# S4 convolution gated by a LoRA feed-forward: the first block's loads on two queues, 20 identity products instead of 24, and VectorE sums at other places of the order

## The chip, the cores and the metric

The kernel runs on one core of one Trainium2 chip, in float32. The metric is the device time of one execution in microseconds (us). A core has TensorE (PE in the profile; its weight loads are PEld), VectorE (DVE), ScalarE (ACT), GpSimd (POOL) and SyncE (SP), whose queue issues most of the DMAs here. ScalarE has a DMA queue of its own. Each engine works through its own list of instructions in order and waits on semaphores.

## The reference, cut to what matters

```python
# x: (2, 1024, 512); w1, w3: (1376, 512); w2: (512, 1376); LoRA rank 16, scale 2
xn = layernorm(x)                                   # no affine, eps 1e-5
s = causal_conv(xn, K) + D * xn                     # along the last axis; K of 512 taps from the S4 state
h1 = xn @ w1.T + 2 * (xn @ A1.T) @ B1.T
h3 = xn @ w3.T + 2 * (xn @ A3.T) @ B3.T
g = silu(h1) * h3
f = g @ w2.T + 2 * (g @ A2.T) @ B2.T
out = x + s * silu(f)
```

The convolution runs over the 512 features of a token, so as a matrix it is a 512 x 512 Toeplitz matrix. Its taps K come from a Cauchy sum at 512 roots and an inverse Fourier transform, computed in the kernel from small inputs.

## The kernel before

**Tiling.** The 2048 tokens are four blocks of 512 tokens, each loaded as four tiles of 128 x 512. A block is normalized (bn_stats and bn_aggr on VectorE for blocks 0 to 2, ScalarE sums for block 3, then one scale and shift per row on ScalarE and GpSimd) and transposed on TensorE into `xr` and `b12`, with ScalarE copying the transposes out of PSUM.

**First product.** `h1` and `h3` are made with a two-level Strassen-Winograd scheme. The 1376 hidden columns are five pairs of 256 columns (`c` = 0 to 4) and a rest of 96 (`last`). A pair has seven inner products, its chains (`j` = 1, 2, 6, 7, 5, 3, 4 in that order), and each chain has seven steps of two 128x512 matmul instructions. The LoRA term is added to the weights first: a rank 16 product into PSUM (`lora_product`, L381) and a VectorE merge (L391). VectorE makes the sums of weights (`inner_weight_sum`, L451, written S1 to S4 in the scheme, into `s[5]`, `s[6]`, `s[7]`, `s[3]`) and of tokens, and adds each chain's second PSUM accumulation to a snapshot that ScalarE has copied out (`Chain.total`, L778). A `y` bank of PSUM that a chain goes on accumulating in, or that a later chain takes over, is free once that total has read it. GpSimd adds and multiplies results (L868, L835), and the gated `g` goes to DRAM.

**Second product.** `f` is made in eight units of 128 tokens per half (`u` = 0 to 7), two to a group of `g`, one level of Strassen-Winograd. A group's sums (`group_piece`, L1176, eight VectorE instructions) are dropped between the steps of the units before. Units 2 and 3 run while the third group's sums are made, while its `g` comes from DRAM, and while VectorE works off the S4 chain (`s4_work`: `s4_resolvent`, `s4_roots`, `s4_matrix`): a Cauchy resolvent `den`, roots on TensorE (L639) read by L648, small complex arithmetic on 128x4 tiles (L655), the operands `z` of the transform (L688, L690) and their products on TensorE (L709). The convolution of the later units (`conv_product`, L928) needs its result.

**Order.** The order on PE, DVE, ACT and POOL is written out by hand: a heap of places (`at`, `after`) is emptied in order for the first product, where one unit of a place is one step of a chain, and `run` goes through the second product. `run` lets two units take turns; after each step it takes one entry of `parts` and then, from the step `s4_from` on, `s4_steps` entries of `s4_work`. An entry `nothing` does nothing and takes one turn.

**The start.** `load_x(0)` issues the four tiles of block 0 on SP; the LoRA factors for `w1` and `w3` (`lo_d`, `lo_h`, 16 rows each) go out on ScalarE's queue at the same time. SP goes on with block 1, the weights of `last`, the first pair's weights, blocks 2 and 3 and the second pair's weights. Each DMA uses one of eight semaphores in turn, so the ninth waits for the landing of the first. TensorE meanwhile multiplies the identity with itself (`keep_warm`, L989: 24 products, two instructions each), then makes the LoRA products of `last` (`lora_last`, L381), ten more identity instructions, and the transposes of block 0 (L303).

Of the kernel before, what the change touches and what calls it, by code (L numbers as in the profile page):

```python
# [17 lines left out]
P = 128  # L18
# [3 lines left out]
HID = 1376  # L22
# [4 lines left out]
TB = 512  # L27
# [6 lines left out]
LSPLIT = 6 * P  # L34
# [73 lines left out]
def s4_gated_ffn(  # L108
# [39 lines left out]
    nc = tc.nc  # L148
# [19 lines left out]
    def bank(tag, borrow=False):  # L168

        i = turn[tag]  # L170
        if not borrow:
            turn[tag] = 1 - i
        return psum.tile([P, 512], F32, tag=f"{tag}{i}", name=tag, bufs=1)
# [36 lines left out]
    def value(tag="s"):  # L210
        return upool.tile([P, TB], F32, tag=tag, name=tag, bufs={"s": 10, "c": 4}[tag])
# [4 lines left out]
    def at(place, what):  # L216
        heapq.heappush(events, (place, next(count), what))
# [7 lines left out]
    def load_x(b):  # L225
        room = (None, None, t_in[4], t_in[6])[b]
        tiles = []
        for tt in range(NTT):
            t = value() if room is None else room[:, tt, :]
            nc.sync.dma_start(out=t, in_=x[bass.ds(b * TB + tt * P, P), :])  # L230
            tiles.append(t)
        return tiles

# [133 lines left out]
    def load_lora(queue, group, d, h, lo, hi):  # L367
        rows = slice(32 * group, 32 * group + R)
        if d is not None:
            queue.dma_start(out=lora["d"][rows, :], in_=d)  # L370
        queue.dma_start(out=lora["h"][rows, : hi - lo], in_=h[:, lo:hi])
        lora["base"][group] = lo
# [21 lines left out]
    def load_pair(c):  # L394
        w = wpool.tile([P, 8, 2, 2, P], F32, tag="w", name="w")
        for v, src in enumerate((w1T, w3T)):
            for half in range(2):
                slot = (1, 2, 0, 3)[2 * v + half]
                rows = src[half * HALF : (half + 1) * HALF, PAIR_AT[c] : PAIR_AT[c] + 2 * P]
                nc.sync.dma_start(  # L400
                    out=w[:, slot].rearrange("p k m h -> p k (m h)"),
                    in_=rows.rearrange("(k p) h -> p k h", p=P),
                )
        return w
# [12 lines left out]
    def merge_whole_pair(c, w, first=None, delays=(1.15, 2.3, 4.3, 4.4)):  # L417

        ps = [first or [bank("y", True), bank("w", True)], [bank("aux"), bank("aux")]]
        for half in range(2):  # L420
            for k in range(2):
                for v in range(2):
                    n = slice(half * 2 * P, (half + 1) * 2 * P)
                    lora_product(
                        ps[k][v][:, n], 2 * k + v, 2 * half + k, PAIR_AT[c], 2 * P, half == 0
                    )
        for (k, v), when in zip(((0, 0), (0, 1), (1, 0), (1, 1)), delays):
            to = w[:, (slice(1, 3), slice(0, 4, 3))[v], k].rearrange("p s m h -> p s (m h)")
            from_ = ps[k][v].rearrange("p (s n) -> p s n", s=2)
            after(when, lambda to=to, from_=from_: merge(to, from_))  # L430

    def outer_weight_sums(w, names):
        a21, a11, a12, a22, s1, s2, s3, s4_ = (
            w[:, i].rearrange("p k m h -> p (k m h)") for i in range(8)
        )
        sums = {1: (s1, a21, a22, add), 2: (s2, a22, s3, sub), 3: (s3, a11, a21, sub)}
        sums[4] = (s4_, a12, s2, sub)
        for name in names:
            nc.vector.tensor_tensor(*sums[name])  # L439

    def inner_weight_sum(w, s, name):
        a11, a12, a21, a22 = (w[:, 1:, k, m, :] for m in range(2) for k in range(2))
        j = {1: 5, 2: 6, 3: 7, 4: 3}[name]
        s[j] = upool.tile([P, 7, P], F32, tag=f"s{j}", name=f"s{j}")
        first, second, op = {
            1: (a21, a22, add),
            2: (s.get(5), a11, sub),
            3: (a11, a21, sub),
            4: (a12, s.get(6), sub),
        }[name]  # L450
        nc.vector.tensor_tensor(s[j], first, second, op)  # L451
# [21 lines left out]
    def lora_last():  # L473
        ps = [bank("y"), bank("y")]
        for dc in range(NDC):
            for v in range(2):
                lora_product(
                    ps[v][:, dc * LASTR : (dc + 1) * LASTR], v, dc, LAST * P, LASTR
                )
        return ps  # L480
# [283 lines left out]
    class Chain:  # L764
# [16 lines left out]
        def step(self, i):  # L781

            rows = self.rows
            if i == 1:
                self.x = bank("x")[:rows, :]
            elif i == 7:
                self.y = bank("y")[:rows, :]
            to = self.w if i == 2 else self.y if i in (7, 4) else self.x
            product(to, self.pairs(i), i in (1, 7), self.parts if i == 1 else 1)
            if i == 1:  # L790
                self.w = bank("w")[:rows, :]
                nc.scalar.copy(self.w, self.x)  # L792
            elif i == 2:
                after(1.2 + self.late, lambda: self.got(11, self.w))
            elif i == 6:
                self.s2 = self.snapshot(21)
            elif i == 5:
                s4_ = self.snapshot(22)
                after(2.1 + self.late, lambda: self.total(22, s4_))
            elif i == 3:  # L800
                after(1.2 + self.late, lambda: self.got(12, self.x))
            elif i == 4:
                after(1.2 + self.late, lambda: self.total(21, self.s2))
# [163 lines left out]
    lora_tiles(LSPLIT)  # L967
    factors = (a1, b1T), (a3, b3T)
    for v, f in enumerate(factors):
        load_lora(nc.scalar, v, *f, LSPLIT, HID)  # L970
    nc.scalar.activation(warm, warm, AF.Silu)
    x_in[1] = load_x(1)
    make_upper_triangular(nc, tri, 1.0, diag=True)
    w_last, s_last = load_last()
# [12 lines left out]
    def keep_warm(ps, n, first=False):  # L987
        for i in range(n):
            nc.tensor.matmul(  # L989
                ps[:, i % 4 * P : (i % 4 + 1) * P],  # L990
                lhsT=ident,
                rhs=ident,
                start=first and i == 0,
                stop=True,
                skip_group_check=True,
            )

    primed = bank("w"), bank("w")
    for ps in primed:
        keep_warm(ps, 12, True)  # L1000
    ps_last = lora_last()
    mv = norm_tile(0)
    norm_stats(0, range(NTT))
# [73 lines left out]
    for n, place in enumerate((12.1, 12.8, 13.7, 14.4)):  # L1077
        b, i = divmod(n, 2)
# [19 lines left out]
    for c in range(NPAIR):  # L1098
        t0 = 14 + 49 * c

        def ready(j):

            n = orders[c].index(j)
            return 7 * (n + (2 if c == 0 and n > 1 else 0)) + (0 if c == 0 else t0) + 13.3

        if c + 1 < NPAIR:
            nx = c + 1

            def step(what, *args, nx=nx):
                return lambda: what(nx, w_pair[nx], *args)  # L1110

            if c > 0:
                at(t0 + 7.5, lambda nx=nx: w_pair.update({nx: load_pair(nx)}))
            t1 = t0 + (24 if c == 0 else 16)
            if c == 0:
                at(
                    5.7,
                    lambda nx=nx: merge_whole_pair(
                        nx, w_pair[nx], [bank("w"), bank("w")], (1.6, 2.6, 4.8, 5.8)
                    ),  # L1120
                )
            else:
                at(t0 + 15.6, step(merge_whole_pair))
            for n, name in enumerate((3, 2, 1, 4)):
                at(
                    14.5 + 0.2 * n if c == 0 else t1 + 8.5 + 1.5 * n,
                    lambda nx=nx, name=name: outer_weight_sums(w_pair[nx], (name,)),
                )
            for name, when in (
                (3, ready(7)),  # L1130
                (1, ready(5)),
                (2, ready(5) + 4),
                (4, max(ready(3), ready(5) + 8)),
            ):
                at(
                    when,
                    lambda nx=nx, name=name: inner_weight_sum(w_pair[nx], s_pair[nx], name),
                )
        else:
            at(t0 - 20, load_w2_factors)  # L1140
            at(t0 + 5, load_w2)
            for n, when in enumerate((15.6, 22.6, 29.6)):
                at(t0 + when, lambda n=n: merge_down(n))
# [303 lines left out]
    after_, more = following(1)  # L1447
    nothing = [lambda: None]
# [36 lines left out]
    def hold(u):  # L1485
# [5 lines left out]
    after_, more = following(2)  # L1491
    hold(HOLD)
    run(
        [unit(2, read), unit(3, read)],
        [*nothing * 2, *more],
        8,
    )
    for _ in s4_work:
# [1 line left out]
    for u in range(HOLD, UNITS):  # L1500
# [9 lines left out]
        more = ()  # L1510
        if u == HOLD:
            more = nothing + [lambda of=of: [part() for part in of] for of in block_sums_[2:]]
        if ahead and j == 1:
            after_, more = following(grp + 1)
# [77 lines left out]
```

## Time and profile before

| | us |
| --- | --- |
| median of 3 runs | 445.49 |
| lowest and highest run | 444.5 and 445.88 |
| profiled execution, device time | 446.04 |
| its span, first to last instruction | 444.2 |

The profiled execution lies 1.84 us over its own span, and 0.55 us above the median of the runs. Over the whole span TensorE is busy for 437.1 us, VectorE for 318.0, GpSimd for 206.1 and ScalarE for 144.6; 53.61 MB go through the DMA queues. A line of the timeline gives start, duration, engine, source line, operation, what is written and read, and how many instructions are merged in it; the bracket tells how long the engine was idle before, and what ended that. "busy" for TensorE includes the time in which its pipeline drains, so small losses show as a longer distance between starts and not as idle time.

### The profile page before, as it was taken

To read this page: it belongs to the slowest core of one execution; us is meant where nothing else is said; L and a number is where in the kernel's file an instruction comes from. 1 tells how busy PE (TensorE), PEld (TensorE's weight loads), DVE (VectorE), ACT (ScalarE), POOL (GpSimd) and SP (SyncE) were. 2 spreads that over 40 slices of the span, in tenths; PEclk is the share of its full clock that TensorE was granted. 3 is DMA by queue.
4 is the path that set the end of the run, shared out by engine and by line. 5 is a ranking of instruction groups with operands and counts; after the bars stand their busy time and mean duration, and the time that the engine had idled before them with its cause. 6 is when DMAs were issued, how large, how long until landed. Compare 5 with 4: busy or idle time off the path is not lost.

```text
span 444.2 us, 5192 instructions
## 1 busy us (share of the span) xinstructions
PE 437.1 (98%) x1722; PEld 271.8 (61%) x1722; DVE 318.0 (72%) x534; ACT 144.6 (33%) x296; POOL 206.1 (46%) x156
## 2 busy tenths in 40 slices
PE   8999999999999999999999999999999999999996
PEld 8645333344444444444443447888888999999995
DVE  5799999955984687468745796979595885653234
ACT  2676332543254325532453242111101212212221
POOL 2306469895669467945794469400000122222221
PEclk9999999999999999999999999999999999999999
DMA  8911304025102500260036526395901843323211
GB/s 263 364 51 38 136 0 147 0 76 174 37 24 72 165 24 24 76 180 25 24 123 209 163 91 213 106 357 187 346 19 72 281 141 96 142 95 96 78 65 48
DMA packets 35466, 53.61 MB, mean 121 GB/s; under 512 B 4688, under 2 KB 21520, under 8 KB 35312
## 3 DMA queue, kind: packets, MB, share of 16 engines
q1 hardware_dynamic: 35312, 53.14, 36.6%
q8 instruction: 13, 0.21, 0.2%
q10 hardware_dynamic: 128, 0.14, 0.1%
q14 instruction: 13, 0.11, 0.1%
HBM read 33.88 MB, written 19.40 MB: 120 GB/s over the span
## 4 chain that ended last, share of the span: by engine, by line
PE 70%; DVE 18%; DMA 7%; issue 2%; ACT 1%; SPq 1%; DVEq 0%; ACTq 0%
PE x L754 35%; PE y L754 18%; PE w L754 9%; PE aux L928 4%; PE w L928 2%; DVE xt L327 2%; DVE s L1176 2%; DVE w L439 1%; DMA t_in<-g_dram 1%; DMA g<-g_dram 1%; DMA t_in<-in_x_dram 1%; DMA lo_h<-in_b1T_dram 1%; DMA w<-in_w1T_dram 1%; DVE t_in L341 1%; DVE s L451 1%
## 5 line engine op out<-in xcount | busy, mean ns | idle before, releaser
L1310 POOL TENSOR_TENSOR o<-o,xin 128x512 f32<-128x512 f32 (+1 forms) x17 | 23.3, 1370 | 134.3 <-DVE o L1309 134.3
L835 POOL TENSOR_TENSOR s<-c,s 128x512 f32<-128x512 f32 (+1 forms) x44 | 63.2, 1441 | 16.5 <-ACT c L827 11.3
L774 ACT COPY s<-x 128x512 f32<-128x512 f32 (+1 forms) x54 | 31.6, 586 | 87.0 <-PE x L754 85.6
L754 PE MATMUL x<-t_in,s 128*128 128x512 f32 (+1 forms) x148 | 55.2, 500 | 0.0
L778 DVE TENSOR_TENSOR s<-s,y 128x512 f32<-128x512 f32 (+1 forms) x54 | 36.1, 679 | 16.4 <-PE y L754 10.9
L868 POOL TENSOR_TENSOR s<-ua_three,s 128x512 f32<-128x512 f32 x20 | 35.9, 1793 | 23.7 <-DVE s L778 23.7
L754 PEld LDWEIGHTS x<-t_in,s 128*128 128x128 f32 x148 | 26.8, 190 | 22.8 <-issue 12.0
L868 POOL TENSOR_TENSOR ua_three<-ua_three,s 128x512 f32<-128x512 f32 x20 | 33.1, 1653 | 14.8 <-DVE s L778 14.8
L754 PE MATMUL y<-t_in,s 128*128 128x256 f32 (+1 forms) x108 | 35.9, 459 | 0.0
L1332 ACT COPY z<-x 128x256 f32<-128x256 f32 x24 | 8.8, 371 | 70.4 <-PE x L754 70.3
L1307 DVE TENSOR_TENSOR aux<-aux,m 128x384 f32<-128x384 f32 x32 | 18.1, 565 | 15.9 <-PE aux L928 14.3
L868 POOL TENSOR_TENSOR s<-u_three,s 128x512 f32<-128x512 f32 x20 | 28.5, 1426 | 1.8 <-ACT c L827 1.0
L827 ACT ACTIVATE c<-c 128x512 f32<-128x512 f32 x40 | 25.2, 632 | 9.6 <-DVE c L868 9.6
L754 PEld LDWEIGHTS y<-t_in,s 128*128 128x128 f32 x108 | 20.1, 190 | 11.3 <-issue 8.8
L792 ACT COPY w<-x 128x512 f32<-128x512 f32 (+1 forms) x37 | 21.1, 570 | 12.5 <-PE x L754 12.4
L754 PE MATMUL x<-t_in,w 128*128 128x512 f32 x40 | 20.9, 603 | 0.0
L754 PE MATMUL x<-xr,w 128*128 128x512 f32 x40 | 20.6, 614 | 0.1
L868 POOL TENSOR_TENSOR u_three<-ua_three,u_three 128x512 f32<-128x512 f32 x10 | 12.7, 1272 | 17.1 <-DVE u_three L778 17.0
L754 PE MATMUL x<-xr,s 128*128 128x512 f32 x40 | 20.6, 616 | 0.1
L754 PE MATMUL x<-xt,w 128*128 128x512 f32 x40 | 20.6, 597 | 0.0
L754 PE MATMUL x<-xt,s 128*128 128x512 f32 x40 | 20.4, 592 | 0.0
L754 PE MATMUL y<-xt,s 128*128 128x512 f32 x40 | 20.0, 597 | 0.4 <-DVE u_three L778 0.4
(302 smaller groups left out, 914.0 us busy)
## 6 DMA issues: line engine op xcount, KB each, us to landing
g_dram<-s SPq DMA_DIRECT2D x40, 256.0 KB, 2.2
g<-g_dram SPq DMA_DIRECT2D x10, 512.0 KB, 5.9
xin<-in_x_dram SPq DMA_DIRECT2D x16, 256.0 KB, 2.8
out_dram<-o SPq DMA_DIRECT2D x14, 256.0 KB, 2.0
t_in<-g_dram SPq DMA_DIRECT2D x6, 512.0 KB, 4.2
w<-in_w1T_dram SPq DMA_DIRECT2D x10, 256.0 KB, 3.3
w<-in_w3T_dram SPq DMA_DIRECT2D x10, 256.0 KB, 4.3
s<-in_x_dram SPq DMA_DIRECT2D x8, 256.0 KB, 4.1
```

Source lines behind the costliest of these rows:

```text
L327: nc.vector.tensor_tensor(to, a, b, add if name == 2 else sub)
L754: nc.tensor.matmul(ps[:, cols], lhsT=lhsT, rhs=rhs if parts == 1 else rhs[:, cols], start=first and i == 0 and part == 0, stop=i == len(pa ...
L774: nc.scalar.copy(t, self.x)
L778: nc.vector.tensor_tensor(t, t, self.y, add)
L792: nc.scalar.copy(self.w, self.x)
L827: nc.scalar.activation(c, c if src is None else src, AF.Silu)
L835: nc.gpsimd.tensor_tensor(g, act, g, mult)
L868: (nc.vector if o < 20 else nc.gpsimd).tensor_tensor(to, a, b, add)
L928: nc.tensor.matmul(to[:, n * P : (n + 1) * P], lhsT=x_, rhs=by, start=start, stop=True, skip_group_check=True,)
L1176: lambda t=t, op=op: nc.vector.tensor_tensor(*t, op)
L1307: nc.vector.tensor_tensor(y[:, P:], y[:, P:], m[:, n * P : (n + 3) * P], add)
L1310: (nc.vector if last else nc.gpsimd).tensor_tensor(o, o, self.xin[h][:, cols], add)
```

## The change

- In `load_x`, tiles 1 and 3 of block 0 are issued on ScalarE's queue, tiles 0 and 2 stay on SP.
- The LoRA factors `a1` and `b1T` go to SP's queue, behind those two tiles; `a3` and `b3T` stay on ScalarE's queue, behind the other two.
- Each of the two opening runs of identity products has 10 instead of 12.
- S3 of the next pair (name 3, into `s[7]`) is placed at `ready(7) + 1.2` instead of `ready(7)`. In the built order it then stands behind one `Chain.total` (L778 `u_three`) and not ahead of it, in four places (pairs 0 to 3).
- While units 2 and 3 run, four empty turns instead of two come ahead of the third group's eight sums. In the built order of VectorE each of them stands further back among the S4 steps: the first one, which stood ahead of L648, comes 14 instructions later, and the last now stands in the midst of `s4_matrix`, ahead of the product with `tri`.

The order of the instructions on TensorE changes in nothing but the eight instructions that are left out, and on GpSimd and ScalarE's compute not at all.

```diff
@@ load_x @@
             t = value() if room is None else room[:, tt, :]
-            nc.sync.dma_start(out=t, in_=x[bass.ds(b * TB + tt * P, P), :])
+            queue = nc.scalar if b == 0 and tt % 2 else nc.sync
+            queue.dma_start(out=t, in_=x[bass.ds(b * TB + tt * P, P), :])
             tiles.append(t)
@@
     for v, f in enumerate(factors):
-        load_lora(nc.scalar, v, *f, LSPLIT, HID)
+        load_lora((nc.sync, nc.scalar)[v], v, *f, LSPLIT, HID)
     nc.scalar.activation(warm, warm, AF.Silu)
@@
     for ps in primed:
-        keep_warm(ps, 12, True)
+        keep_warm(ps, 10, True)
@@
             for name, when in (
-                (3, ready(7)),
+                (3, ready(7) + 1.2),
                 (1, ready(5)),
@@
     run(
         [unit(2, read), unit(3, read)],
-        [*nothing * 2, *more],
+        [*nothing * 4, *more],
         8,
     )
```

## Prediction, before the changed kernel was run

> **What bounds the kernel now.** I read the page first, then the busy time by stage, and then the timeline at the three places that the change touches.
>
> ```profile
> PE 437.1 (98%) x1722; PEld 271.8 (61%) x1722; DVE 318.0 (72%) x534; ACT 144.6 (33%) x296; POOL 206.1 (46%) x156
> ```
>
> ```profile
> 22.60:90.30 67.70, 66.97 (x195) 28.61 (x196) 65.69 (x83) 32.46 (x67) 41.92 (x24) 1.00 0.20 65
> 90.30:255.00 164.70, 164.70 (x433) 68.26 (x433) 110.42 (x150) 64.76 (x114) 112.31 (x84) 1.00 0.29 92
> 255.00:344.20 89.20, 88.49 (x386) 69.73 (x385) 70.78 (x162) 16.41 (x36) 22.11 (x15) 1.00 0.52 174
> ```
>
> TensorE (first column after the length) is never off the path for long, so only what lets TensorE start sooner or stand still less can count. From 22.6 to 90.3 VectorE (third) is full too, 65.69 of 67.70 us, so a gain ahead of 22.6 must reach both. Later VectorE has a third of its time free. The timeline of the start:
>
> ```profile
> 1.37 8.52 PE L989 MATMUL w<-ident 128*128 128x128 f32 x48 [1.37 <-POOL ident masks.py:199]
> ...
> 3.73 0.69 DVE L246 BATCH_NORM_STATS2 stats<-s 128x6 f32<-128x512 f32 x1 [3.73 <-DMA s<-in_x_dram]
> ...
> 9.72 1.52 ACT L292 ACTIVATE s<-s,shift,rs_y 128x512 f32<-128x512 f32 x2 [5.65 <-DVE shift L283]
> ...
> 9.82 1.13 PE L381 MATMUL y<-lo_h,lo_d 16*128 16x96 f32 x16
> ...
> 12.10 1.04 PE L303 MATMUL aux<-ident,s 128*128 128x128 f32 x8
> ...
> 17.46 1.29 DVE L391 SCALAR_TENSOR_TENSOR w<-aux,w 128x512 f32<-128x512 f32 x2 [1.62 <-PE aux L381]
> ...
> 22.59 1.29 DVE L327 TENSOR_TENSOR xt<-xr,b 128x512 f32<-128x512 f32 x2 [0.64 <-ACT xr L314]
> ```
>
> The first two normalized tiles are ready about 10.55 (9.72 and half of 1.52, and the like on GpSimd), but their transposes start at 12.10: TensorE's own list is late, not the data. VectorE then waits for it (1.62 us before 17.46), and for the transposes of block 1 (0.64 before 22.59). Next, the first pair, and units 2 and 3:
>
> ```profile
> 77.16 2.32 DVE L343 TENSOR_TENSOR t_in<-xt,t_in 128x2048 f32<-128x2048 f32 x1
> 77.28 3.32 POOL L868 TENSOR_TENSOR ua_three<-ua_three,s 128x512 f32<-128x512 f32 x1
> ...
> 79.40 2.15 DVE L451 TENSOR_TENSOR s<-w 128x896 f32<-128x896 f32 x1
> ...
> 81.48 0.67 DVE L778 TENSOR_TENSOR u_three<-u_three,y 128x512 f32<-128x512 f32 x1
> 82.07 0.67 DVE L778 TENSOR_TENSOR s<-s,y 128x512 f32<-128x512 f32 x1
> ...
> 82.20 1.98 PE L754 MATMUL y<-xt,s 128*128 128x512 f32 x4 [0.35 <-DVE u_three L778]
> ```
>
> ```profile
> 317.13 0.96 DVE L1176 TENSOR_TENSOR s<-t_in 128x768 f32<-128x768 f32 x1 [4.20 <-DMA t_in<-g_dram]
> 318.00 0.18 DVE L648 COPY k<-aux 128x32 f32<-128x32 f32 x1
> ...
> 331.72 0.49 PE L709 MATMUL aux<-room 128*128 128x128 f32 x2 [0.66 <-DVE room L690]
> ```
>
> In the first, S3 (79.40) stands ahead of the total that frees a `y` bank, and TensorE waits for that total. In the second, the first sum of the third group holds VectorE for 4.20 us for a DMA; L648, whose roots were done at 313.43, sits behind it, and the S4 chain then reaches TensorE late.
>
> **The change part by part.** The sum is made against the profiled execution, 446.04 us (span 444.2 and 1.84 around it), 0.55 above the median of the runs.
>
> *Identity products.* Of 48 instructions, 28 start in the first 5.92 us (0.213 us apart), and from 7.5 on they are 0.112 apart (10 take 1.12 us after 10.88). The four products left out are eight of the fast ones: 8 x 0.112 = 0.89 us. The transposes then come at 11.2, still 0.65 after their data. Followed on: the copy L792 moves from 16.40 to 15.5 and block 1's normalization behind it from 16.88 to 16.0 (its shift was ready at 15.37); L391 moves from 17.46 to 16.6, with its predecessor done at 15.84; the stretch from 22.59 starts 0.89 earlier on both engines. Its later loads are in time: block 2's tiles were waited for by no row, the second pair's weights are merged only after 33 us. So -0.89; the ends are 0 (data late) and -1.70 (eight at 0.213).
>
> The Trainium skill ("TensorE: Matmul & The Clock Gate", section "What's actually happening") says that the clock rises after some 3.4 us of busy time, in a window that doesn't start with the kernel, so that the number of slow instructions differs from run to run. The trace shows about 6 us, and it shows one run. By that rule the gain would differ between runs; that is a rival below.
>
> *Two queues, LoRA behind.* VectorE's first three statistics waited for tiles, at 3.73, 4.85 and 5.96, 1.11 us apart with the LoRA rows between them; from 6.0 to 8.5 us the queues move 385 GB/s, 0.68 us a tile. Interleaved, tiles 0 and 1 should land together near 4.4, and tiles 2 and 3 by 5.8 (3.71 and three times 0.68). Four statistics of 0.83 from 4.4 end at 7.7, as now (7.70): nothing. Ends: -0.4 (the two waits of 0.2 gone) and +0.5 (first tile at 4.85). Both are hidden by the 0.65 us that the data still lead by. The factors landed 4.3 us after the last issue, at 6.4; TensorE wants them at 8.9, so 2.5 us cover their place behind 512 KB (1.4 us). SP sheds two issues and takes two; block 1's tiles were read at 9.61 with no wait, and the weights of `last` (10.3 by 5.95 and 4.3) have 0.9 us to their merge at 11.22. If that cover went, TensorE would wait for the excess. I take 0.
>
> *S3 behind the total.* The total now runs at 79.40 and frees its bank at 80.07; TensorE wanted it at 81.69 and got it at 82.20. With the restart (0.534 instead of 0.43 between starts) that is 0.51 + 0.10 = 0.62 us. Behind S3 now waits the other total (82.07), which the second product in `y` wants at 82.45. S3's 2.15 is 1.09 of work and a wait for GpSimd's add, which ended at 80.60; it should again start at 80.6, end by 81.6, and the total by 82.3: in time. In pairs 1 to 3 no such wait shows, so 0. Total -0.62; ends -0.62 and +0.45 (below).
>
> *Third group's sums.* L648 goes at 313.45. Five small steps (0.64) on, unit 3's L1353 waits for its product until 316.2 and ends at 316.5. From there to L688 the trace has 5.61 us with three sums (2.35) in it; three of 768 columns (2.61) make it 5.87, to 322.4. The Fourier table lands at 322.6 (issued 314.34, 8.3 us). From L688 to the `z` that TensorE waits for it was 6.22; with one sum of 768 more (0.87) it is 7.1 less what leaves it, a sum of 512 (0.6): 6.5, so 329.2. TensorE wants it at 330.9. The 24 instructions of L709 took 3.86 us from 329.79 to 333.65, at 0.111 they take 2.66: -1.20. The sums themselves end by about 337, and unit 4 wants its first one after 348. Ends: 0 and -1.20.
>
> Sum: 0.89 + 0.62 + 1.20 = 2.71; 446.04 - 2.71 = 443.33, and from the median 445.49 - 2.71 = 442.8.
>
> **Rivals.** *The data bound the start.* If the clock had risen at 4.1 instead of 7.4, fifteen instructions would take 0.1 us less, the transposes would stand at 10.6 in the kernel before already, and leaving products out brings nothing: 445.49 - 1.82 = 443.7. For it: the lowest run lies 1.5 us under the profiled one. Against it: the one trace. 0.15.
>
> *GpSimd goes first.* The total that now comes early frees GpSimd's next add at 80.1. If that add takes its turn at 80.6 ahead of S3, S3 ends at 82.9, the other total at 83.5, and TensorE is 0.45 later than before instead of 0.62 earlier: 445.49 - 1.64 = 443.85. By the Trainium skill ("SBUF — State Buffer", section "Who interferes with whom") such a pair excludes each other for whole instructions, and the first to issue wins. Against it: at 87.55 and 90.92 a waiting L451 went ahead of GpSimd's next add. 0.08.
>
> *The S4 chain stays late,* held by the table or by L1353: without the 1.20 it is 444.0. Against it: 1.7 us to spare. 0.08.
>
> *Absorbed:* two of the three fail, or later waits take them up: about 445. 0.12.
>
> *Block 0 lands late (slower).* Two queues may slow both, and the block's last tile comes later. TensorE's lead over the data was 1.5 us and the last tile landed by 6.79; from 8.3 on each us costs one. It outweighs the other two gains (1.82) beyond 10.1, and makes the kernel slower by over 0.3% beyond 11.5; at 12 it is 447.4. For it: the Trainium skill ("DMA: Bandwidth & Descriptors", section "Issuing engines are not separate DMA queues") has all queues on the same engines, so a second one adds no rate. Against it: 1 MB at 385 GB/s is 2.7 us. 0.05.
>
> **How the numbers follow.** The forecast, all three gains, has 0.52: 442.8. A measurement of this kernel tells about 0.3%, 1.34 us, from no change. One gain missing leaves 1.5 to 2.1 us, mostly still beyond that: 0.52 and some 0.22 of the 0.31 make 0.74 for faster; the rest of these and the absorbed case 0.19; slower 0.07. The range goes down to 442.0 (eight slow instructions, 1.70 for 0.89) and up to 444.9, which leaves out some 0.17 above.
>
> **What would show it.** Right: 40 instructions of L989 and L303 at 11.2; no wait in front of TensorE's `y` product near 81 less 0.9; L648 directly behind the roots, and L709 in one run of 2.7 us. Wrong: L381 or L303 waiting for a DMA or for L283; S3 still running when `y` is wanted; L709 split again; or these gone and new waits of the same size before 90 us.

## The result, and the profile after

The changed kernel takes 442.60 us in the median of 6 runs (441.96 to 442.73), beside 445.17 for the kernel before (6 runs, 444.5 to 445.88). The ratio is 0.9939 with a 95% interval of 0.9924 to 0.9954: 2.7 us less, between 2.0 and 3.4. The profiled execution took 442.51 us with a span of 440.7, which is 3.5 less than the profiled execution before. Most of the difference between 2.7 and 3.5 belongs to the one execution that was profiled before: it lies 0.87 us above the median of its kernel, and the experiments show where. Lines past the first edit carry numbers that are one higher in this profile (L303 is L304, L709 is L710).

The page first, engine totals:

```profile
PE 434.7 (99%) x1714; PEld 270.7 (61%) x1714; DVE 315.0 (71%) x534; ACT 144.6 (33%) x296; POOL 209.3 (47%) x156
```

Eight instructions fewer on TensorE, and still nothing but TensorE that matters in the sum. Busy time by stage (after the length: TensorE, its weight loads, VectorE, ScalarE, GpSimd):

```profile
22.60:90.30 67.70, 67.33 (x191) 28.59 (x192) 65.28 (x84) 31.96 (x68) 44.48 (x26) 1.00 0.20 66
...
255.00:341.50 86.50, 86.50 (x385) 69.50 (x384) 70.12 (x162) 16.59 (x37) 22.06 (x15) 1.00 0.52 178
```

The gap of TensorE in the first stage has shrunk, and in the last one it is gone. The timeline of the start (start, duration, engine, line, operation, number of instructions, and in brackets the idle time before and what ended it):

```profile
1.37 7.41 PE L990 MATMUL w<-ident 128*128 128x128 f32 x40 [1.37 <-POOL ident masks.py:199]
...
3.98 0.69 DVE L247 BATCH_NORM_STATS2 stats<-s 128x6 f32<-128x512 f32 x1 [3.98 <-DMA s<-in_x_dram]
...
5.93 0.69 DVE L247 BATCH_NORM_STATS2 stats<-s 128x6 f32<-128x512 f32 x1 [0.24 <-DMA s<-in_x_dram]
...
9.65 1.52 ACT L293 ACTIVATE s<-s,shift,rs_y 128x512 f32<-128x512 f32 x2 [5.57 <-DVE shift L284]
...
10.99 1.04 PE L304 MATMUL aux<-ident,s 128*128 128x128 f32 x8
...
11.82 0.56 DVE L392 SCALAR_TENSOR_TENSOR last<-y,last 128x384 f32<-128x384 f32 x1 [0.58 <-DMA last<-in_w1T_dram]
...
16.01 1.52 ACT L293 ACTIVATE s<-s,shift,rs_y 128x512 f32<-128x512 f32 x2 [0.16 <-DVE shift L284]
...
16.37 1.28 DVE L392 SCALAR_TENSOR_TENSOR w<-aux,w 128x512 f32<-128x512 f32 x2
...
21.48 1.29 DVE L328 TENSOR_TENSOR xt<-xr,b 128x512 f32<-128x512 f32 x2 [0.63 <-ACT xr L315]
```

The transposes start at 10.99 instead of 12.10, again behind TensorE's own list. A new wait is there, 0.58 us of VectorE for the weights of `last`; TensorE does not feel it: VectorE idled for 1.62 us ahead of L391 in the profile before, and the wait uses that up (at 16.37 no idle time is left). The first pair:

```profile
78.27 0.68 DVE L779 TENSOR_TENSOR u_three<-u_three,y 128x512 f32<-128x512 f32 x1
...
78.86 1.56 DVE L452 TENSOR_TENSOR s<-w 128x896 f32<-128x896 f32 x1
...
79.55 2.00 POOL L869 TENSOR_TENSOR u_three<-ua_three,u_three 128x512 f32<-128x512 f32 x1
...
80.35 0.67 DVE L779 TENSOR_TENSOR s<-s,y 128x512 f32<-128x512 f32 x1
80.56 1.88 PE L755 MATMUL y<-xt,s 128*128 128x512 f32 x4
```

The total is ahead of S3, the product into `y` has no wait, and S3 (78.86) went ahead of GpSimd's next add (79.55). VectorE in units 2 and 3, with the first and the last instructions of L710 on TensorE and what follows them there:

```profile
311.16 0.19 DVE L649 COPY k<-aux 128x32 f32<-128x32 f32 x1 [0.42 <-PE aux L640]
...
313.93 0.42 DVE L1354 TENSOR_TENSOR o<-z,w 128x256 f32<-128x256 f32 x1 [2.03 <-PE w L755]
...
315.24 0.96 DVE L1177 TENSOR_TENSOR s<-t_in 128x768 f32<-128x768 f32 x1
...
320.18 0.29 DVE L689 TENSOR_SCALAR conv<-room,ai 128x128 f32<-128x128 f32 x1
...
326.92 0.35 DVE L691 SCALAR_TENSOR_TENSOR room<-room,ar,conv 128x128 f32<-128x128 f32 x1
...
327.48 0.39 PE L710 MATMUL aux<-room 128*128 128x128 f32 x2
...
329.93 0.39 PE L710 MATMUL aux<-room,t_in 128*128 128x128 f32 x2
330.15 1.89 PE L755 MATMUL x<-w_a,s 128*128 128x256 f32 x8
```

L649 follows directly on the roots, the wait of 4.20 us for a DMA is gone, and of the idle time 2.03 us are left in front of unit 3's own copy. L710 on TensorE (L709 before) now runs from 327.48 to 330.15 without a break, 2.67 us.

Laid side by side, the starts of TensorE's instructions in the two profiles drift apart at these places only: 1.11 us by the end of the identity products, 0.64 at the `y` product (82.20 before), 1.18 at L709, and 0.56 in small steps at 239.9, 302.6 and 312.4, which no part of the forecast accounts for. Together 3.49.

### The profile page after: what moved, and what is told of

It is laid out like the page before. It is cut to its first block, busy times and chain, and to the rows that moved or that the text cites. A ratio compares the mean times of both kernels' runs of the same rounds, so it can differ in the third digit from the quotient of the medians.

```text
span 440.7 us, 5176 instructions
## 1 busy us (share of the span) xinstructions
PE 434.7 (99%) x1714; PEld 270.7 (61%) x1714; DVE 315.0 (71%) x534; ACT 144.6 (33%) x296; POOL 209.3 (47%) x156
## 4 chain that ended last, share of the span: by engine, by line
PE 89%; DMA 4%; DVE 4%; ACT 1%; SPq 1%; issue 1%; ACTq 0%; DVEq 0%
PE x L755 44%; PE y L755 23%; PE w L755 12%; PE aux L929 4%; PE w L929 2%; DMA w<-in_w3T_dram 1%; DMA t_in<-in_x_dram 1%; DMA s<-in_x_dram 1%; DVE xt L328 1%; PE aux L304 1%; PE y L382 1%; PE y L528 1%; PE aux L710 1%; DVE w L440 1%; DMA lo_h<-in_b3T_dram 1%
## 5 line engine op out<-in xcount | busy, mean ns | idle before, releaser
L779 DVE TENSOR_TENSOR s<-s,y 128x512 f32<-128x512 f32 (+1 forms) x54 | 36.1, 680 | 17.5 <-PE y L755 12.1
L869 POOL TENSOR_TENSOR u_three<-ua_three,u_three 128x512 f32<-128x512 f32 x10 | 15.6, 1557 | 12.8 <-DVE u_three L779 12.7
L755 PE MATMUL y<-xt,w 128*128 128x512 f32 x40 | 19.8, 594 | 0.1
```

The source lines that it names most:

```text
L755: nc.tensor.matmul(ps[:, cols], lhsT=lhsT, rhs=rhs if parts == 1 else rhs[:, cols], start=first and i == 0 and part == 0, stop=i == len(pa ...
L779: nc.vector.tensor_tensor(t, t, self.y, add)
L869: (nc.vector if o < 20 else nc.gpsimd).tensor_tensor(to, a, b, add)
```

## The experiments

Each kernel was timed in five rounds against the kernel before on the same chip; an unchanged copy of the kernel before was profiled once more, without timing rounds. The last column is the ratio less one, multiplied by 445.3 us, with its 95% interval.

| kernel | median us | ratio and 95% interval | us against before |
| --- | --- | --- | --- |
| two queues alone | 445.01 | 1.0001 (0.9990 to 1.0011) | 0.0 |
| 20 products alone | 444.85 | 0.9990 (0.9977 to 1.0002) | -0.4 (-1.0 to +0.1) |
| S3 alone | 444.39 | 0.9981 (0.9967 to 0.9995) | -0.8 (-1.5 to -0.2) |
| sums alone | 444.30 | 0.9982 (0.9970 to 0.9993) | -0.8 (-1.3 to -0.3) |
| S3 and sums | 443.61 | 0.9960 (0.9945 to 0.9974) | -1.8 (-2.4 to -1.2) |
| all but the queues | 442.56 | 0.9943 (0.9927 to 0.9960) | -2.5 (-3.3 to -1.8) |
| all | 442.60 | 0.9939 (0.9924 to 0.9954) | -2.7 (-3.4 to -2.0) |
| all, 16 products | 442.49 | 0.9941 (0.9924 to 0.9958) | -2.6 (-3.4 to -1.9) |
| all, 18 products | 442.58 | 0.9941 (0.9924 to 0.9957) | -2.6 (-3.4 to -1.9) |
| all, 28 products | 444.11 | 0.9976 (0.9966 to 0.9987) | -1.1 (-1.5 to -0.6) |
| all, 3 empty turns | 442.84 | 0.9944 (0.9930 to 0.9958) | -2.5 (-3.1 to -1.9) |
| all, 6 empty turns | 442.68 | 0.9941 (0.9927 to 0.9956) | -2.6 (-3.3 to -2.0) |

**The two queues alone.**

```diff
-            nc.sync.dma_start(out=t, in_=x[bass.ds(b * TB + tt * P, P), :])
+            queue = nc.scalar if b == 0 and tt % 2 else nc.sync
+            queue.dma_start(out=t, in_=x[bass.ds(b * TB + tt * P, P), :])
...
-        load_lora(nc.scalar, v, *f, LSPLIT, HID)
+        load_lora((nc.sync, nc.scalar)[v], v, *f, LSPLIT, HID)
```

> Of the change, only the two queues for block 0 and the LoRA factors behind it. Theory (each part of the change works at a wait of its own, and TensorE's own list of 48 identity products sets the start): no gain, 445.2 us within 0.4, because the transposes of block 0 still start near 12.1, behind the list; tiles at about 4.0, 4.1, 5.9 and 6.4, statistics ended by 7.7 as before, and a wait of VectorE of about 0.5 us for the weights of last near 11.7 that TensorE does not feel, since VectorE idled 1.62 us ahead of L391 before. Rival (the queues are the part that makes the start shorter): transposes before 11.8 and at most 444.7. Rival (the later weights of last and tiles of block 1 are felt): 445.6 or more, with VectorE or TensorE waiting for them before 22.6.

No gain and no loss, as the theory had it. But the transposes stood at 10.84 in this profile, not at 12.1, with all 48 instructions in front of them, and that would have spoken for the first rival, had the time followed. It did not: the other profiles below show the same in kernels that have one queue. The wait for `last` was not there (its weights landed at 10.58).

**20 products alone.**

```diff
-        keep_warm(ps, 12, True)
+        keep_warm(ps, 10, True)
```

> Of the change, only the 20 identity products instead of 24. Theory: 445.2 - 0.9 = 444.3 us (0.2 either way for the moment at which the clock rises): 40 instructions, transposes of block 0 at 11.2 and no wait of TensorE ahead of them, because the LoRA factors landed by 6.44 in the old order and the tiles by 6.8. Rival (the earlier TensorE needs the new queues): L381 or L303 waits for a DMA or for the data, and 445.0 or more. Rival (the two queues made the clock rise 0.44 us earlier in the changed kernel): the first fast product at 7.5 again, and the gain 0.2 smaller than in the whole change.

-0.4 us, with zero just inside the interval: half of what was expected. The profile shows nothing wrong, with 40 instructions, no wait ahead of L381 or L303, and the transposes at 10.68. So the start was not held up by data here. The small gain fits a kernel before that often starts sooner than in its first profile; the second profile of it and the table further down show that it does. All 11 runs lie within 0.75 us (444.55 to 445.30), those of the kernel before within 3.0 (35 runs, 443.93 to 446.92).

**S3 alone.**

```diff
-                (3, ready(7)),
+                (3, ready(7) + 1.2),
```

> Of the change, only the place of S3 behind the first total. Theory: 445.2 - 0.6 = 444.6 us: the total of u_three ahead of L451, no wait of TensorE ahead of the y product near 81.7, nothing in pairs 1 to 3. Rival (GpSimd's next add takes its turn ahead of S3): L451 ends near 82.9, TensorE waits about 1 us for the second total, 445.6. Rival (taken up later): the wait gone, but 445.2, with a new wait of 0.5 us or more for VectorE between 82 and 90.

The theory holds, in place and in size. Against the first profile of before, TensorE gains 0.51 us at this `y` product and 0.11 at the next instruction, and nothing is given back by 90 us. The total comes first, S3 next, GpSimd's add after that.

**The sums alone.**

```diff
-        [*nothing * 2, *more],
+        [*nothing * 4, *more],
```

> Of the change, only four empty turns ahead of the third group's sums instead of two. Theory: 445.2 - 1.2 = 444.0 us: L648 directly behind the roots near 313.5, L709 in one run of about 2.7 us instead of 3.86. If the 0.56 us that the changed kernel gained at 239.9, 302.6 and 312.4 beyond the forecast come from this part (the planner places other steps of the third group earlier too), it is 443.5 or less; if they are a matter of the single profiled run, they are absent here or appear without any change of order at those places. Rival (the chain stays late by the Fourier table or by unit 3's own copy): 444.9 or more, with L709 still split.

-0.8 us by the times (to -1.3), and 1.18 us between 331.7 and 332.7 in the comparison with the first profile: 0.82 and three restarts. The theory holds in its mechanism; the times can't tell 0.8 from 1.2. At 239.9 and 302.6, where this kernel changes nothing, it loses 0.18 and gains 0.06 against the first profile.

**The kernel before, again.** An unchanged copy.

> The kernel before, unchanged, for a second profile of it. Theory (the moment of the rise belongs to the run, not to the order of the instructions): the clock rises somewhere between 4.9 and 7.5 us, and the transposes start 0.48 us earlier per us of earlier rise than 12.10 at 7.50; TensorE's wait of 0.35 us for the u_three total near 82 and the split L709 are there again; the three small gains of the changed kernel near 239.9, 302.6 and 312.4 (0.56 us together) are there without any change, if they belong to the first profile. Rival (they belong to the change): the shifts at 239.9, 302.6 and 312.4 are as in the first profile of before.

444.78 us, 1.26 below the first profiled execution of the same instructions. Most of that, 1.11 us, arises before 13 us. Windows of one microsecond, of the first profile of before and of this one (after the length: TensorE and its instructions, weight loads, VectorE, ScalarE, GpSimd; then granted TensorE clock, DMA share, GB/s):

```profile
5.00:6.00 1.00, 1.00 (x6) 1.00 (x6) 0.77 (x3) 0.00 (x0) 0.00 (x0) 1.00 1.05 281
```

```profile
5.00:6.00 1.00, 1.00 (x12) 1.00 (x11) 0.81 (x2) 0.00 (x0) 0.00 (x0) 1.00 1.06 278
```

Between 5 and 6 us one run does 6 identity instructions and the other 12. The step from 0.213 to 0.112 us between starts comes at 7.50 us in the one and at 4.52 in the other. "The rise" here means this step. The view prints a granted clock of 1.00 in both, but in the first run it has nothing to go by: the packed trace keeps the granted clock as records, the first of them (1.00) begins at 7.48 us there and at 4.55 in the second run, and the view prints 1.00 where there is no record. And then the other limit shows (timeline of the second profile):

```profile
9.49 1.38 PE L989 MATMUL w<-ident 128*128 128x128 f32 x10
10.07 1.52 ACT L292 ACTIVATE s<-s,shift,rs_y 128x512 f32<-128x512 f32 x2 [6.00 <-DVE shift L283]
...
10.94 1.09 PE L303 MATMUL aux<-ident,s 128*128 128x128 f32 x8
```

Ten instructions from 9.49 at 0.112 would let the transposes start near 10.7. They start at 10.94, right after ScalarE has finished the first of its two tiles at 10.88: in this run the data bound the start even with 48 products. TensorE's wait for the total (0.35 us, at 81.07 in this profile), a wait of 4.15 us ahead of the third group's sums, and the split L709 are all there again. Against the first profile, steps of 0.07 and 0.21 us at 239.9 and 302.6 are there without any change of the kernel, so half of the 0.56 belongs to the first profile.

**All but the queues.** The changed kernel with the first diff above undone.

> The changed kernel with one part undone: block 0 in one queue and the LoRA factors ahead of it again; 20 products, S3 and sums as changed. Theory (the queues are worth nothing in time): 442.6 us within 0.3, no wait of TensorE ahead of the transposes of block 0, and VectorE's wait of 0.58 us for the weights of last gone. Rival (20 products want the earlier tiles or the later factors): 443.2 us or more, with a wait ahead of L381 or L303. Rival (the weights of last are felt): 442.2 or less.

442.56 us: the queues are worth nothing that five rounds can show, and their loss of cover for `last` costs nothing. L381 (8.37) and L303 (10.65) have no wait.

**16 and 18 products.** `keep_warm(ps, 8, True)` and `keep_warm(ps, 9, True)` in the changed kernel.

> The changed kernel with 16 identity products instead of 20 (32 instructions ahead of the first work). The six profiles so far have the rise of the clock at 4.89, 5.33, 6.19, 6.41, 7.05 and 7.50 us, and the transposes of block 0, in the four with 48 instructions, at 10.84, 11.05, 11.47 and 12.10. The first two normalized tiles are ready near 10.4. Theory (the moment of the rise differs from run to run, and data ready at 10.4 are a floor): the transposes wait for their data and start near 10.5 whatever the moment of the rise; 0.5 to 0.7 less than 20 products on a late rise, nothing on an early one, so 442.3 us in the median, and the runs lie closer together than those of the kernel before (spread 3.0 us in 35 runs; changed kernel 0.8 in 6). Rival (fewer products delay the rise): fast from 8 us on or later, transposes after 11.2, 443.0 or more. Rival (each product counts in full, 0.22 us): 441.7.

> The changed kernel with 18 identity products instead of 20. Theory (floor of the data at 10.4): transposes at 10.5 to 10.75, 442.4 us in the median, between the changed kernel and that with 16, and no more than 0.1 above 16. Rival (each product counts in full): 442.15, and 16 products 0.45 below it. Rival (the rise is delayed): 442.8 or more.

442.49 and 442.58 us. If each product counted in full, they would be at 441.7 and 442.15; they are where 20 products are, within 0.1. The floor of the data is there to see, in the timeline with 16:

```profile
10.45 1.09 PE L304 MATMUL aux<-ident,s 128*128 128x128 f32 x8 [0.37 <-ACT s L293]
```

In it, TensorE waits 0.37 us for the normalized tile (0.43 with 18 products). It also waits 0.88 for the LoRA factors at 7.48, which costs nothing, as it comes ahead of the other wait. That the runs lie closer together than with 20 products is not shown: the spread is 1.1 and 0.5 us beside 0.8. The rise came at 4.31 and 5.96, so fewer products do not put it off.

**S3 and sums without the start.** The first two diffs undone in the changed kernel.

> The changed kernel without its two edits of the start: one queue, LoRA factors first, 24 products; S3 and the third group's sums as changed. Theory (the later two parts add up at their forecast size, 0.62 + 1.20 = 1.82): 445.2 - 1.8 = 443.4 us, within 0.4; what is missing to the changed kernel (442.6) is the products' part, 0.5 to 0.9. Rival (the parts need each other, or one takes up the other): 444.2 or more, or 442.8 or less.

443.61 us, 1.8 less than before: the two parts add up as forecast (1.82), and the start's share of the whole change is what is left: 0.9 by the ratios, 443.61 - 442.60 = 1.0 us by the medians, beside 0.4 for the products alone. The intervals in the table are too wide to tell these apart.

**28 products.** `keep_warm(ps, 14, True)` in the changed kernel.

> The changed kernel with 28 identity products instead of 20, that is 16 instructions more, well beyond the floor of the data. Theory (above the floor a product costs its full price and TensorE's start passes one to one to the end): transposes at 11.7 to 13.0 by the moment of the rise (0.89 behind the 10.84 to 12.10 of 48 instructions), some 1.4 us behind the changed kernel, 444.0 us, and the runs spread over 1 us or more. Rival (VectorE, full until 90 us, sets the end and gives part of it back): 443.3 or less.

444.11 us, 1.5 above the changed kernel, as expected, with the transposes at 11.88. Where TensorE's list is the limit, its start passes on one to one, and VectorE gives nothing back: this profile is 0.89 us behind that of the changed kernel at the transposes and still 0.9 at 300 us.

**Three and six empty turns.** `[*nothing * 3, *more]` and `[*nothing * 6, *more]` in the changed kernel.

> The changed kernel with three empty turns instead of four: the first sum of the third group behind the second L1354 by one step instead of eight, at about 314.35, where its data landed at 314.40 in the changed kernel. Theory (what counts is that the chain of L656 is not held): hardly any wait for the data, but the fourth sum of 768 columns, 0.95 us, comes ahead of the Fourier steps; TensorE had nothing to wait for at 327.48 with 0.2 us to spare, so L710 is split again and 0.5 to 0.7 us are lost: 443.2 us. Rival (the price of the old order was the wait of 4.20 us alone): 442.6.

> The changed kernel with six empty turns instead of four: all the sums of the third group later, two sums of 768 columns fewer ahead of the Fourier steps. Theory (L710 already runs without a wait in the changed kernel, so TensorE's own list sets this place): no gain, 442.6 us within 0.3, L710 dense again, VectorE's steps ahead of it done a microsecond or two earlier. Rival (VectorE's chain still sets the place): 442.0 or less. Rival (the later sums reach unit 4 too late): 443.0 or more, with a wait of TensorE between 331 and 355.

With three my theory fell: 442.84 us, where 443.2 was expected, and in the profile L710 starts at 326.98 and is dense. The first sum waits a little, the fourth one does come ahead of the Fourier steps, and it doesn't matter (timeline of VectorE, and the start of L710):

```profile
314.16 0.96 DVE L1177 TENSOR_TENSOR s<-t_in 128x768 f32<-128x768 f32 x1 [0.31 <-DMA t_in<-g_dram]
...
319.58 0.95 DVE L1177 TENSOR_TENSOR s<-t_in,s 128x768 f32<-128x768 f32 x1
...
326.98 0.38 PE L710 MATMUL aux<-room 128*128 128x128 f32 x2
...
327.48 0.35 DVE L691 SCALAR_TENSOR_TENSOR t_in<-room,ai,conv 128x128 f32<-128x128 f32 x1
```

The last operand is written at 327.83, 0.85 us after L710 has begun, and L710 is dense all the same. In the kernel that operand is first read by the eighth of L710's 12 products, which at two instructions each and 0.111 us apart starts some 1.55 us behind the first; so the 0.2 us that I had counted up to the first instruction were not the limit. Against the wait of 4.20 us, which this order does not have either, the place of the fourth sum is worth nothing. With six, 442.68 us and no gain, as expected: VectorE's chain only gets to wait elsewhere, for the Fourier table.

```profile
321.01 0.28 DVE L689 TENSOR_SCALAR conv<-room,ai 128x128 f32<-128x128 f32 x1 [2.20 <-DMA room<-in_dft_dram]
```

None of these kernels is faster than the changed one by more than the runs can tell.

## Why the prediction was right, point by point

**The total.** 2.71 us were forecast and 2.7 (2.0 to 3.4) measured; 442.8 and 442.6 in the medians. The three mechanisms are there, but one of the three terms took a single profile for the rule, and its size holds only for runs like that one. So the agreement to the hundredth is luck: with 0.69 for that term, the mean that is worked out below, the sum is 2.5, and the parts timed alone add up to 2.0 (0.4, 0.8 and 0.8), both within what the intervals allow.

**Identity products: right where the rise is late, too large in the mean.** 0.89 was worked out from "the one trace", in which the step to the fast spacing came at 7.50 us. That is the latest of the 14 profiles there are now:

| profile | instructions ahead | rise | list done (worked out) | first tile ready | transposes |
| --- | --- | --- | --- | --- | --- |
| before, first | 48 | 7.50 | 12.10 | 10.54 | 12.10 |
| S3 and sums | 48 | 6.80 | 11.77 | 11.10 | 11.74 |
| S3 alone | 48 | 6.19 | 11.48 | 10.66 | 11.47 |
| sums alone | 48 | 5.33 | 11.07 | 10.74 | 11.05 |
| queues alone | 48 | 4.89 | 10.86 | 10.19 | 10.84 |
| before, again | 48 | 4.52 | 10.68 | 10.88 | 10.94 |
| 28 products | 56 | 5.15 | 11.87 | 10.12 | 11.88 |
| changed kernel | 40 | 7.05 | 11.00 | 10.47 | 10.99 |
| 20 products alone | 40 | 6.41 | 10.69 | 10.51 | 10.68 |
| all but the queues | 40 | 6.38 | 10.68 | 10.60 | 10.65 |
| 6 empty turns | 40 | 4.68 | 9.87 | 10.77 | 10.82 |
| 3 empty turns | 40 | 4.29 | 9.69 | 10.14 | 10.20 |
| 18 products | 36 | 5.96 | 10.04 | 10.55 | 10.60 |
| 16 products | 32 | 4.31 | 8.81 | 10.39 | 10.45 |

(All in us. The list is worked out from the first row: each us of earlier rise saves 1 - 0.112/0.213 = 0.475 us, each instruction 0.111. "First tile ready" is the end of ScalarE's first normalization of block 0. With 16 products the list also waits 0.88 us for the LoRA factors, which 8.81 leaves out.) In every row the transposes start at the later of the two limits, within 0.06 us. The mean start is 11.36 with 48 instructions (six profiles) and 10.67 with 40 (five): 0.69 us, between the 0.4 and the 1.0 that the timed kernels gave (both means mix kernels with one and with two queues). A late rise makes the gain 0.89; at the earliest the list with 48 is already at the data's limit, and the gain is nothing. Leaving out eight more instructions gained 0.1 us by the medians, which the runs can't tell from nothing: on an early rise the data are the limit already, and on a late one 0.5 us are left to gain (10.99 and 10.47 in the changed kernel's profile). The profile-to-profile gain of 1.11 was 0.89 and 0.475 x 0.45 = 0.21 from a rise 0.45 us earlier.

**The rival that the data bound the start** was thus not refuted, it is what happens in the runs with an early rise. I had put it down as one world or the other (0.15); which of the two limits holds differs from run to run. Its sign in the profile, transposes behind the normalized tile and not behind L989, is in 4 of the 7 profiles with 40 instructions or fewer, and in one with 48. The rule named with it, of the Trainium skill ("TensorE: Matmul & The Clock Gate", section "What's actually happening"), that the window is free-running with 3.4 us, so that the number of slow instructions differs from run to run, agrees with the range of the rise: 4.29 to 7.50, 3.2 us wide. A rise 2.9 us after the first instruction (4.29 - 1.37) is sooner than a whole window. That it is the clock which rises, the traces show: in each of the 14 the first record of the granted clock, 1.00, begins within 0.09 us of the rise, and a record of 0.5 follows at the end of the run. The record of 1.00 lasts 436.906 us in ten profiles and 433.493 in the other four, 3.413 us apart and 128 and 127 times some 3.413 us, so the clock changes on a grid of that step.

**Two queues: 0, right; its working partly not.** Tiles 0 and 1 landed at 3.96 and 4.14, not together near 4.4, and the last one at 6.39, not by 5.8; the statistics still ended at 7.64 (7.7 forecast). The cover of 0.9 us for the weights of `last` was too small: they landed at 11.72, and VectorE waited 0.58. In the seven profiles with two queues they landed between 10.31 and 11.75, and the wait shows in two (0.58 and 0.54, the latter with 18 products). The step that failed is "if that cover went, TensorE would wait for the excess": VectorE's slack behind it (1.62 us before 17.46) took it. A small benefit I had not seen stays without proof in the times: the last tile lands at 6.07 to 6.69 in the seven profiles with two queues and at 6.74 to 7.22 in the seven with one, and the first tile is normalized at 10.12 to 10.77 and at 10.51 to 11.10. That moves only the data's limit.

**S3 behind the total: right to the hundredth.** 0.51 and 0.10 forecast; 0.51 and 0.10 between the second profile of before and the changed kernel, where the start is level (0.00). GpSimd did not go first: S3 took its turn at the end of GpSimd's 3.31 us add, and the add at 79.55 took 2.00 us, where one of the same shape at 74.92 took 1.28; it ended 1.13 us after S3. These rows agree with the rule cited with the rival ("SBUF — State Buffer", section "Who interferes with whom" of the Trainium skill): whole instructions in turn, with VectorE as the first to issue.

**Third group's sums: right.** 1.20 forecast; 1.18 against the first profile of before and 1.14 (from 0.87 to 2.01) against the second. L710 took 2.67 us (2.66 forecast). The first instruction of L710 was not the one that set the time to spare, as the kernel with three turns showed.

**Block 0 late (the slower rival):** the last tile landed at 6.39, 1.9 us ahead of the 8.3 from which it would have counted.

**What the forecast left out.** The 0.56 us in small steps: 0.07 and 0.21 of them come and go between two profiles of the same kernel. Some 0.2 more, at 302.9 and 312.4, separate the changed kernel's profile from the second one of before too, but are not in the profiles with 16 products, with six turns and with one queue, which have the same order there, so they go with the run too; I have not followed them to a cause.

## What to carry to other kernels

A term worked out from the first microseconds needs a second profile of the same kernel: in the six profiles with 48 instructions of warm-up the start of the transposes differed by 1.26 us, more than the whole gain of that edit. Where two limits lie 1.5 us apart in one profile, ask how far each moves from run to run, and take the mean of the later of the two, not the difference in the one profile. A wait that holds an in-order engine for data (S3, the sums) is worth what its slot costs downstream, and the time to spare behind it is not read from the first instruction that uses the result alone.

## What the runs showed of the hardware

The step from 0.213 to 0.112 us between identity instructions came 2.9 to 6.1 us after TensorE's first one, at a place that showed no relation to the number of instructions (4.52 to 7.50 us with 48, 4.29 to 7.05 with 40). The granted clock's first record begins with it, at 4.26 to 7.48 us, and the column of the views reads 1.00 ahead of it too, where nothing is on record: in the first microseconds the distance between starts tells the clock, not the column. That TensorE idled between the identity products and its first work (0.88 us for the factors with 16 products, after the step) did not bring the slow spacing back: the ten identity instructions behind it took 1.38 us, as in the kernel before.
